# Transposing the first batch's deformable samples on TensorE through score banks

## The chip, the cores and the metric

The kernel runs on one core of one Trainium2 chip. The metric is device time in microseconds (us), lower is better, given as the median of several executions. Five engines work side by side, each with its own in-order queue of instructions: TensorE (PE; PEld is its weight load), VectorE (DVE), ScalarE (ACT), GpSimd (POOL) and SyncE (SP, which in this kernel issues nearly all DMAs). An instruction that waits holds up everything behind it on its engine.

## The reference

Four images of 128 channels and 64 x 64 positions go through two layers.

```python
x = x + deform(_gn(x), ...)                  # layer 0
t = _to_tokens(x)                            # [4, 4096, 128]
t = t + attn(_ln_t(t), ...)                  # layer 1
t = t + experts(_ln_t(t), ...)
...
# deform: offsets and a mask by two 3x3 convolutions, a bilinear sample of
# 128 channels at 9 shifted places per position, times the mask, then
out = jnp.einsum('bckhw,ock->bohw', samples, w_flat)
# attn: q = k = v = products of cosines of the 16 heads' 8 numbers
scores = jnp.einsum('bhsd,bhtd->bhst', q, q) / np.sqrt(D)
ctx = jnp.einsum('bhst,bhtd->bhsd', jax.nn.softmax(scores, axis=-1), q)
# then a projection, layer norms and a small feed-forward
# experts: softmax router over 8, the best two of them, weighted sum
```

All inputs and outputs are float32.

## The kernel before

**Tiling.** A batch is one image. Its 4096 positions are 8 *chunks* of 512 (`CH`), its 16 heads 4 groups of 4 (`NGRP`). A *run* is one (batch, group, query chunk) over a list of key blocks of 128; a *step* is one key block of a run. A step has four score matmuls (`scores`, L1261, into two tiles of the pool `ps_s`, each 2 x 512 columns wide; that pool has three such tiles, called score banks below), two exponentials on ScalarE (L1270) and four matmuls into the accumulator `acc` (`context`, L1281). Scores are issued two steps ahead of the sums (`LAG`). There are 3700 steps; some blocks of exponentials are not computed anew but turned by VectorE and handed to another chunk by way of DRAM (`turn` L1140, `etd`, L1214).

**Side work.** Around the steps two kinds of jobs run, as Python generators. `prepare(b)` makes keys and values of a batch: group norm, a table of image corners in DRAM, offsets (`offsets`), then `deform`. Its 96 *units*, 12 for each chunk (3 groups of taps x 4 blocks of 128 positions), each gather three taps by indirect DMA from POOL (L625), then multiply and add on VectorE (L645, L650, L651). `convolved` takes a chunk's 9 x 512 samples, channels on partitions (`sT`), and multiplies them with the weights (L754 to L757 by way of the helper line L281, 18 products of 256 columns), and `features` turns the result into queries, keys (`kTd`, `qTd`) and values (`fqd`) in DRAM, from where runs load them (L1239, L1241, L1249). `finish(b, ch)` is the rest of the network for a chunk whose sums are done: `attention_out`, `feed_forward`, `experts`. Two `finish` jobs may be open; they have rank 1 and 2.

**Samples.** Samples come with positions on partitions and have to be transposed. Batch 0's chunks 0 and 1 (`ch < 2`) take TensorE: three transposes into the one bank `misc`, held until VectorE copies it (L665) after the next unit's product. All others take a detour: VectorE transposes squares of 32 (L686) into `tr9`, SyncE stores that to `smd` in DRAM (L698, four stores for each group of taps) and loads it back in the other order (L731, `get`).

**The order of instructions** on PE, DVE, POOL and SP is written out by a planner in the kernel, the class `Beside`. It keeps its own clock (`now`, 1.82 us a step) and a time at which VectorE will be free (`dve`). A generator yields what it needs next (PE time, VectorE time, a delay); `step` emits it when it fits: VectorE's queue is no longer than `backlog`, a share `rate` of PE time has been saved up, at most `fills` jobs with PE work a step, and the bank `misc` is free, which `hold=True` reserves, and `hold=None` ignores. `later` emits a DMA at a due time. `force` runs a job when the next step's keys aren't there. After the last step `drain` emits what is left, one job to its end before the next.

**The opening.** In batch 0 the steps start before all chunks are prepared. The first 26 runs (`opening`, 160 steps; the flag `streaming`) work on the chunks 0 to 3 as they come: chunk 1 is wanted from step 16, chunk 2 from 64, chunk 3 from 104, chunks 4 to 7 from step 256. Partial sums are therefore parked in DRAM: at a run's end ScalarE copies `acc` to `cu` (L1491), SyncE stores it to `partd` 3 us later by the planner's clock (`park_sums`, L1126), and a later run of the same sums loads it at its first step (L1456) and adds it by four matmuls with the identity (L281, `acc<-cu`).

Of the kernel before, what the change touches and what calls it, by code (L numbers as in the profile page):

```python
# [22 lines left out]
P = 128  # L23
# [195 lines left out]
def tr(n):  # L219

    return 0.13 + 0.115 * n
# [3 lines left out]
def kernel(  # L225
# [373 lines left out]
    def deform(b, tab, idx, wt, rest):  # L599
# [7 lines left out]

        def early(n):

            return b == 0 and n < 3 * 12  # L610

        def gather(last):

# [20 lines left out]
        for n, (ch, kg, j) in enumerate(units):  # L634
            progress[b] = 0.1 + 0.9 * n / len(units)
            if b == 0 and n == 36:
                yield need(dve=5.0)
                settle()
            while not ahead:
                yield need(lat=0.5)  # L640
            v, landed = ahead.pop(0)
            v4 = v.rearrange("p k (q c) -> p (k q) c", c=C)
            w12 = wt[:, j, 3 * kg : 3 * kg + 3, :].rearrange("p k q -> p (k q)")
            yield need(dve=ve(1536), after=landed)
            nc.vector.tensor_tensor(v4, v4, w12[:, :, None].to_broadcast([P, 12, C]), ALU.mult)  # L645
            if moved:
                yield need(pe=0.01, dve=ve(384))
                moved.pop()()
            yield need(dve=ve(768) + ve(384))
            nc.vector.tensor_tensor(v[:, :, : 2 * C], v[:, :, : 2 * C], v[:, :, 2 * C :], ALU.add)  # L650
            nc.vector.tensor_tensor(v[:, :, :C], v[:, :, :C], v[:, :, C : 2 * C], ALU.add)  # L651
            if b == 0 and ch < 2:


                if n % 12 == 0:
                    while len(summed) < ch:
                        yield need(lat=0.5)
                    sT = big.tile([P, KK, CH], F32, tag="xs", name=f"sT_first{ch}")
                yield need(pe=tr(3), lat=FREE, hold=True)
                pt = misc(f"sT_ps{j}_{kg}")  # L660
                for k in range(3):
                    nc.tensor.transpose(pt[:, P * k : P * (k + 1)], v[:, k, :C], ident)

                def move(sT=sT, kg=kg, i=j % 4, pt=pt):
                    nc.vector.tensor_copy(  # L665
                        sT[:, 3 * kg : 3 * kg + 3, P * i : P * (i + 1)],
                        pt[:, : 3 * P].rearrange("p (k c) -> p k c", c=P),
                    )

                moved.append(move)  # L670
                beside.later(beside.now + 0.8, lambda n=n: gather(n))
                if n % 12 == 11:
                    yield need(pe=0.01, dve=ve(384))
                    moved.pop()()
                    featuring.append(True)
                    beside.add("prepare", convolved(b, ch, sT), 0.5, True)
                    if ch == 0:
                        yield from rest
                continue

            yield need(dve=ve(384))
            if j % 4 == 0:
                beside.flush(sent)
                tr9 = work.tile([P, 4, 4, 4, 32], F32, tag="st", name=f"tr{b}_{ch}_{kg}", bufs=NST)
            for k in range(3):
                nc.vector.transpose(  # L686
                    out=tr9[:, k, :, j % 4, :],
                    in_=v[:, k, :C].rearrange("p (c i) -> p c i", i=32),
                )
            beside.later(beside.dve, lambda n=n: gather(n))  # L690
            if j % 4 < 3:
                continue
            while kg == 0 and len(featuring) > 1:
                yield need(lat=1.0)

            def put(ch=ch, kg=kg, tr9=tr9):
                for o in range(4):
                    nc.sync.dma_start(  # L698
                        out=smd[ch % 2][:, 3 * kg : 3 * kg + 3, :, o].rearrange(
                            "i k c n -> i (k c) n"  # L700
                        ),
                        in_=tr9[32 * o : 32 * (o + 1), :3].rearrange("p k c j t -> p (k c) (j t)"),
                    )
# [15 lines left out]
    def convolved(b, ch, sT=None):  # L719
# [4 lines left out]
        if not in_order:  # L724
            yield need(lat=2.5)

            sT = big.tile([P, KK, CH], F32, tag="xs", name=f"sT{b}_{ch}")

        def get(kg):
            for c in range(4):  # L730
                nc.sync.dma_start(  # L731
                    out=sT[32 * c : 32 * (c + 1), 3 * kg : 3 * kg + 3],
                    in_=smd[ch % 2][:, 3 * kg : 3 * kg + 3, c].rearrange("i k o n -> i k (o n)"),
                )

# [5 lines left out]
        for k in range(KK):  # L741
            if k == 2 and not in_order:
                get(2)
            for hf in range(2):
                last = k == KK - 1 and hf == 1
                yield need(pe=MM256, dve=ve(128, 4) if last else 0.0, lat=0.2 if last else FREE, hold=not last)
                if k == 0 and hf == 0:
                    po = misc(f"conv_ps{b}_{ch}")
                by_columns(
                    po[:, 256 * hf : 256 * (hf + 1)], wconv_sb[:, k, :],  # L750
                    sT[:, k, 256 * hf : 256 * (hf + 1)], k == 0 and hf == 0, last,
                )
        summed.append(True)
        for o in range(4):  # L754
# [38 lines left out]
    def features(b, ch, x2, mean, rstd):  # L793
# [55 lines left out]
        beside.later(beside.dve - ve(512), lambda: put(0, hi))  # L849
        beside.later(beside.dve, lambda: put(1, lo))  # L850
        prepared[b, ch] = beside.dve + 9.0
        featuring.pop(0)

# [65 lines left out]

    def feed_forward(b, ch, x4, a4):  # L920

        z3 = [
            work.tile([P, 4, HD], F32, tag=f"zf{k}", name=f"zf{k}{b}_{ch}") for k in range(3)
        ]
# [29 lines left out]
        for i in range(4):  # L954
            for f in range(FFN // P):
# [164 lines left out]

        beside.later(beside.dve, put)

    def park_sums(g, sc, cu, when):

        def put():
            nc.sync.dma_start(out=partd[g][sc], in_=cu)  # L1126
            storing.discard((g, sc))

        storing.add((g, sc))
        beside.later(when, put)  # L1130

# [90 lines left out]

    landing = {}
    fetched = {}
    groups, done, active = {}, [], []

    def finishing():

# [179 lines left out]
    with tc.manual_schedule(engines={PE, DVE, SP, POOL}):  # L1410
# [6 lines left out]
        while n < len(steps):  # L1417
# [17 lines left out]
                    gives.remove(steps[m])  # L1435
                    turn(es[m - n], *steps[m])

            beside.fills = 3 if run < 12 else 1
            if streaming:
                backlog = 1.5  # L1440
            else:
                backlog = 0.4 if at >= len(ts) - 3 else 3.2
            if b + 1 < NB:
# [45 lines left out]
                cu = work.tile([P, 512], F32, tag="cu", name=f"cu{run}", bufs=NCU)  # L1489
            if by_act:  # L1490
                nc.scalar.copy(cu, acc)  # L1491
# [83 lines left out]
```

## Time and profile before

| | us |
|---|---|
| median of 3 executions | 7609.23 (7607.39 to 7621.65) |
| the profiled execution | 7579.71 |
| its span, first to last instruction | 7576.5 |
| ScalarE busy in it | 6863.5 |
| TensorE busy in it, as modelled | 7113.9 |
| first exponential starts at | 176.2 |
| steps 16, 20, 104, 160, 320 start at | 267.5, 287.6, 491.9, 637.0, 954.6 |
| last exponential starts at | 7490.8 |

A profile row has an engine, a line of the code, an operation, `out<-in` by the program's names, a count, and busy time. A row "A <- B: t, n, m" in the list of waits says that A waited for B t us in all, n times, at most m. A timeline row begins with its start and its length; in brackets stands the idle time before it and what ended that. Ends of matmuls are modelled, so TensorE's share looks fuller than it is. Matmuls in full float32 have two records each.

### The profile page before, as it was taken

The page shows a single profiled execution, that of the slowest core. Times are in us where ns is not written, and L with a number is a line of the kernel's source. Part 1 is how long each engine was busy: PE and PEld are TensorE (multiplying, and loading weights), DVE is VectorE, ACT ScalarE, POOL GpSimd, SP SyncE. Part 2 cuts the span into 40 slices and gives each one's busy share as a digit, 9 for nine tenths or more (in the row PEclk, how much of TensorE's full clock was granted, in tenths as well). Part 3 has the DMA queues.
Part 4 walks back from the last instruction along what each step waited for, and adds up shares of the span by engine and source line. Part 5 has one row for each costly group of instructions (what it writes and reads, how often), then busy time and mean ns, then how long its engine had stood idle before and what let it go on. Part 6 is the DMA issues. An engine that isn't in the chain of part 4 may idle for free.

```text
span 7576.5 us, 180754 instructions
## 1 busy us (share of the span) xinstructions
PE 7113.9 (94%) x73848; PEld 2375.9 (31%) x73848; DVE 4465.9 (59%) x8950; ACT 6863.5 (91%) x7467; POOL 1653.2 (22%) x1326
## 2 busy tenths in 40 slices
PE   3688999899999999999999999999999999999997
PEld 2122222223333333333333323333333333333333
DVE  7755356667444877776544677775444554455434
ACT  0578999889999999999999998989999999999995
POOL 5544034443000433422000334431000000000000
PEclk6889999999999999999999999999999999999998
DMA  6777567978446878887655789897454466666661
GB/s 181 223 204 219 141 223 241 300 234 291 149 168 200 292 244 280 268 277 244 203 179 190 228 279 298 289 324 237 174 190 152 148 236 230 232 222 239 226 202 63
DMA packets 909788, 1689.51 MB, mean 223 GB/s; under 512 B 150754, under 2 KB 384124, under 8 KB 858268
## 3 DMA queue, kind: packets, MB, share of 16 engines
q1 hardware_dynamic: 809102, 1371.37, 54.9%
q0 software_dynamic: 92160, 302.06, 12.4%
q8 instruction: 579, 9.49, 0.5%
q10 hardware_dynamic: 7694, 4.52, 0.2%
q14 instruction: 253, 2.07, 0.1%
HBM read 1027.51 MB, written 650.14 MB: 221 GB/s over the span
## 4 chain that ended last, share of the span: by engine, by line
PE 80%; DMA 8%; DVE 4%; issue 2%; ACT 2%; SPq 1%; another core or an unknown queue 0%; POOL 0%; POOLq 0%; DVEq 0%; ACTq 0%
PE acc L1281 39%; PE sc L1261 24%; PE acc L1214 5%; PE e_ps L281 4%; PE conv_ps L281 3%; DMA et<-etd 2%; PE f_ps L281 2%; ACT e L1270 2%; DMA etd<-st 1%; DMA sT<-smd 1%; PE om_ps L533 1%; DMA smd<-tr 1%; DVE st L1140 1%; DVE v L645 1%; DMA cu<-part 1%
## 5 line engine op out<-in xcount | busy, mean ns | idle before, releaser
L1270 ACT ACTIVATE e<-sc 128x1024 f32<-128x1024 f32 x7400 | 6849.4, 1081 | 527.0 <-PE sc L1261 368.1
L1281 PE MATMUL acc<-e,qf 128*9 128x512 f32 (+1 forms) x29600 | 3938.3, 601 | 18.6 <-ACT cu L1491 7.5
L1261 PE MATMUL sc<-qT,kT 32*128 32x512 f32 x14800 | 2368.7, 499 | 153.3 <-ACT e L1270 84.8
L1261 PEld LDWEIGHTS sc<-qT,kT 32*128 32x128 f32 x14800 | 942.8, 183 | 3612.6 <-ACT e L1270 3130.4
L625 POOL DMA_INDIRECT v<-tab,idx x1152 | 1451.8, 1260 | 1579.3 <-DVE tr L686 956.2
L1140 DVE STREAM_TRANSPOSE st<-e 128x1024 f32<-128x1024 f32 x792 | 937.3, 1222 | 752.4 <-ACT e L1270 620.1
L1281 PEld LDWEIGHTS acc<-e,qf 128*9 128x9 f32 (+1 forms) x29600 | 682.4, 91 | 610.3 <-issue 346.8
L396 POOL TENSOR_TENSOR r<-ln_t,expo 128x4 f32<-128x4 f32 x96 | 112.2, 1169 | 3105.4 <-DVE ln_t L394 3057.0
L645 DVE TENSOR_TENSOR v<-v,wt 128x1536 f32<-128x1536 f32 x384 | 667.0, 1737 | 119.5 <-DMA v<-tab,idx 96.8
L1214 PE MATMUL acc<-et,qv 128*9 128x128 f32 x12672 | 506.4, 276 | 52.2 <-DMA et<-etd 44.6
L1065 DVE TENSOR_TENSOR eo<-e_ps,gt 128x512 f32<-128x512 f32 x256 | 175.2, 686 | 552.5 <-PE e_ps L281 547.5
L650 DVE TENSOR_TENSOR v<-v 128x768 f32<-128x768 f32 x384 | 367.2, 956 | 10.1
L281 PE MATMUL conv_ps<-sT,wconv_sb 128*32 128x256 f32 x4320 | 351.0, 399 | 15.7 <-DMA sT<-smd 11.6
L1214 PEld LDWEIGHTS acc<-et,qv 128*9 128x9 f32 x12672 | 270.0, 90 | 254.4 <-issue 212.6
L686 DVE STREAM_TRANSPOSE tr<-v 128x128 f32<-128x128 f32 x1080 | 249.4, 282 | 37.5 <-DMA etd<-st 28.7
L1493 DVE COPY cu<-acc 128x512 f32<-128x512 f32 x116 | 80.2, 692 | 306.3 <-PE acc L1281 260.8
L651 DVE TENSOR_TENSOR v<-v 128x384 f32<-128x384 f32 x384 | 215.7, 562 | 13.3
L396 POOL TENSOR_TENSOR rstd<-lt_t,expo 128x4 f32<-128x4 f32 x32 | 57.9, 1811 | 575.9 <-DVE lt_t L394 550.7
L281 PE MATMUL f_ps<-w_sb,h 128*32 128x128 f32 x4096 | 166.1, 282 | 0.1
L950 DVE TENSOR_SCALAR h<-h_ps,b_sb 128x512 f32<-128x512 f32 x128 | 94.9, 744 | 100.3 <-PE h_ps L948 89.9
L823 POOL COPY fx<-rn 128x512 f32<-128x512 f32 x32 | 26.8, 838 | 526.3 <-DVE rn L822 321.4
L965 DVE TENSOR_TENSOR a<-a,f_ps 128x512 f32<-128x512 f32 x32 | 21.9, 685 | 198.8 <-PE f_ps L281 198.8
(227 smaller groups left out, 3166.9 us busy)
## 6 DMA issues: line engine op xcount, KB each, us to landing
etd<-st SPq DMA_DIRECT2D x396, 1024.0 KB
et<-etd SPq DMA_DIRECT2D x396, 1024.0 KB
kT<-kTd SPq DMA_DIRECT2D x372, 256.0 KB
smd<-tr SPq DMA_DIRECT2D x360, 192.0 KB
sT<-smd SPq DMA_DIRECT2D x360, 192.0 KB
qT<-qTd SPq DMA_DIRECT2D x166, 256.0 KB
atd<-cu SPq DMA_DIRECT2D x128, 256.0 KB
qf<-fqd SPq DMA_DIRECT2D x372, 72.0 KB
```

Source lines behind the costliest of these rows:

```text
L281: nc.tensor.matmul(dst[c : c + 32], lhsT=lhsT[:, c : c + 32], rhs=rhs, start=start, stop=stop)
L625: nc.gpsimd.indirect_dma_start(out=v[:, k, :], out_offset=None, in_=tab, in_offset=bass.IndirectOffsetOnAxis(ap=idx[:, j, kk : kk + 1], ax ...
L645: nc.vector.tensor_tensor(v4, v4, w12[:, :, None].to_broadcast([P, 12, C]), ALU.mult)
L650: nc.vector.tensor_tensor(v[:, :, : 2 * C], v[:, :, : 2 * C], v[:, :, 2 * C :], ALU.add)
L651: nc.vector.tensor_tensor(v[:, :, :C], v[:, :, :C], v[:, :, C : 2 * C], ALU.add)
L686: nc.vector.transpose(out=tr9[:, k, :, j % 4, :], in_=v[:, k, :C].rearrange("p (c i) -> p c i", i=32),)
L1065: nc.vector.tensor_tensor(ws[hf], pe.rearrange("p (e c) -> p e c", c=C), gt[:, i, 4 * hf : 4 * (hf + 1), None].to_broadcast([P, 4, C]), AL ...
L1140: nc.vector.transpose(out=st[:, :, 2 * pr : 2 * pr + 2, :].rearrange("p o h (q j) -> p o (h q) j", j=32), in_=es[pr].rearrange("p h (q o i ...
L1214: nc.tensor.matmul(acc[32 * h : 32 * h + QW, P * kt : P * (kt + 1)], lhsT=qv[:, at : at + QW], rhs=e[:, :, h, 32 * t : 32 * (t + 1)], star ...
L1261: nc.tensor.matmul(ps[i // 2][:, i % 2, :], lhsT=kT[h : h + 32, P * (t % 4) : P * (t % 4 + 1)], rhs=qT[h : h + 32, :], start=True, stop=True,)
L1270: nc.scalar.activation(e, ps[pr], AF.Exp, scale=1.0 / math.sqrt(HD))
L1281: nc.tensor.matmul(acc[32 * h : 32 * h + width, :], lhsT=flat[:, first : first + width], rhs=es[h // 2][:, h % 2, :], start=(t == ts[0]), ...
```

## The change

It has six parts.

1. All of batch 0's samples go through TensorE. The target of the transposes is a score bank of `ps_s` in place of `misc`, and VectorE copies it by three copies of 128 columns. Even chunks' samples lie in the one buffer `xs`, odd chunks' in nine of the eleven buffers `f2` that the finishing jobs use later; a chunk may start when the one two before it is summed.
2. In batch 0 the gathers run 4 units ahead throughout (before: in the first 36 units, 2 later), with the buffers `et` as additional space.
3. While streaming, `fills` is 3 (before: in the first 12 runs) and `backlog` 4.0 (before 1.5).
4. `features`: the values' copy moves from POOL to VectorE; its stores become one DMA for four, and those of keys and queries four for eight, with another order of the rows.
5. While streaming, the parked sums are stored by a DMA that ScalarE issues right after its copy.
6. Only one `feed_forward` at a time may be between its start and its second sum (`heavy`).

```diff
         def early(n):
-            return b == 0 and n < 3 * 12
+            return b == 0
...
             if moved:
-                yield need(pe=0.01, dve=ve(384))
+                yield need(dve=ve(128, 3))
                 moved.pop()()
...
-            if b == 0 and ch < 2:
+            if b == 0:
                 if n % 12 == 0:
-                    while len(summed) < ch:
+                    while len(summed) < ch - 1:
                         yield need(lat=0.5)
-                    sT = big.tile([P, KK, CH], F32, tag="xs", name=f"sT_first{ch}")
-                yield need(pe=tr(3), lat=FREE, hold=True)
-                pt = misc(f"sT_ps{j}_{kg}")
+                    if ch % 2:
+                        sT = [
+                            work.tile([P, CH], F32, tag="f2", name=f"sT{ch}_{k}", bufs=NF2)
+                            for k in range(KK)
+                        ]
+                    else:
+                        sT = big.tile([P, KK, CH], F32, tag="xs", name=f"sT_first{ch}")
+                        sT = [sT[:, k] for k in range(KK)]
+                yield need(pe=tr(3), lat=FREE, hold=None)
+                pt = ps_s.tile([P, 2, 512], F32, tag="sc", name=f"sT_ps{j}_{kg}")[:, 0, :]
                 for k in range(3):
                     nc.tensor.transpose(pt[:, P * k : P * (k + 1)], v[:, k, :C], ident)
                 def move(sT=sT, kg=kg, i=j % 4, pt=pt):
-                    nc.vector.tensor_copy(
-                        sT[:, 3 * kg : 3 * kg + 3, P * i : P * (i + 1)],
-                        pt[:, : 3 * P].rearrange("p (k c) -> p k c", c=P),
-                    )
+                    for k in range(3):
+                        nc.vector.tensor_copy(
+                            sT[3 * kg + k][:, P * i : P * (i + 1)], pt[:, P * k : P * (k + 1)]
+                        )
                 moved.append(move)
                 beside.later(beside.now + 0.8, lambda n=n: gather(n))
                 if n % 12 == 11:
-                    yield need(pe=0.01, dve=ve(384))
+                    yield need(lat=0.6)
+                    yield need(dve=ve(128, 3))
                     moved.pop()()
...
-        beside.later(beside.dve, lambda: nc.gpsimd.tensor_copy(f4[:, :, :, :HD], q8))
-        def put_values():
-            for g in range(NGRP):
-                nc.sync.dma_start(out=fqd[b % 2][ch][g], in_=fx[:, :, QG * g : QG * g + QL])
-        beside.later(beside.dve + 2.0, put_values)
-        yield need(pe=tr(4), dve=ve(512, 2))
+        yield need(pe=tr(4), dve=ve(512, 3))
...
         nc.vector.tensor_tensor(lo.bitcast(F32R), pt, hi, ALU.subtract)
+        nc.vector.tensor_copy(f4[:, :, :, :HD], q8)
         def put(part, fT):
-            kd = kTd[b % 2][ch].rearrange("(h l r d) n -> l r h d n", l=2, r=2, d=HD)
-            qd = qTd[b % 2][ch].rearrange("(h r l d) n -> l r h d n", l=2, r=2, d=HD)
-            for rep in range(2):
-                nc.sync.dma_start(out=kd[part, rep], in_=fT)
-                nc.sync.dma_start(out=qd[part, rep], in_=fT)
+            kd = kTd[b % 2][ch].rearrange("(p l r) n -> l p r n", l=2, r=2)
+            qd = qTd[b % 2][ch].rearrange("(p r l) n -> l p r n", l=2, r=2)
+            twice = fT[:, None, :].to_broadcast([P, 2, CH])
+            nc.sync.dma_start(out=kd[part], in_=twice)
+            nc.sync.dma_start(out=qd[part], in_=twice)
+        def put_values():
+            nc.sync.dma_start(
+                out=fqd[b % 2][ch].rearrange("g p t x -> p t g x"),
+                in_=fx.rearrange("p t (g x) -> p t g x", g=NGRP),
+            )
...
     def feed_forward(b, ch, x4, a4):
+        while heavy:
+            yield need(lat=1.0)
+        heavy.append(True)
...
         nc.vector.tensor_tensor(a4, a4, pf.rearrange("p (i c) -> p i c", c=C), ALU.add)
+        heavy.pop()
...
-            beside.fills = 3 if run < 12 else 1
+            beside.fills = 3 if streaming else 1
             if streaming:
-                backlog = 1.5
+                backlog = 4.0
...
             if by_act:
                 nc.scalar.copy(cu, acc)
+                nc.scalar.dma_start(out=partd[g][sc], in_=cu)
...
-            else:
-                park_sums(g, sc, cu, beside.now + 3.0 if by_act else beside.dve)
+            elif not by_act:
+                park_sums(g, sc, cu)
```

More of the change, by code (lines that the diff above doesn't have):

```diff
@@ L725, in convolved @@
             yield need(lat=2.5)
-            sT = big.tile([P, KK, CH], F32, tag="xs", name=f"sT{b}_{ch}")
+            sTs = big.tile([P, KK, CH], F32, tag="xs", name=f"sT{b}_{ch}")
+            sT = [sTs[:, k] for k in range(KK)]
         def get(kg):
@@ L731, in get @@
                 nc.sync.dma_start(
-                    out=sT[32 * c : 32 * (c + 1), 3 * kg : 3 * kg + 3],
+                    out=sTs[32 * c : 32 * (c + 1), 3 * kg : 3 * kg + 3],
                     in_=smd[ch % 2][:, 3 * kg : 3 * kg + 3, c].rearrange("i k o n -> i k (o n)"),
@@ L750, in convolved @@
                     po[:, 256 * hf : 256 * (hf + 1)], wconv_sb[:, k, :],
-                    sT[:, k, 256 * hf : 256 * (hf + 1)], k == 0 and hf == 0, last,
+                    sT[k][:, 256 * hf : 256 * (hf + 1)], k == 0 and hf == 0, last,
                 )
@@ L839, in features @@
         nc.vector.tensor_tensor(lo.bitcast(F32R), pt, hi, ALU.subtract)
+        nc.vector.tensor_copy(f4[:, :, :, :HD], q8)
         def put(part, fT):
-            kd = kTd[b % 2][ch].rearrange("(h l r d) n -> l r h d n", l=2, r=2, d=HD)
-            qd = qTd[b % 2][ch].rearrange("(h r l d) n -> l r h d n", l=2, r=2, d=HD)
-            for rep in range(2):
-                nc.sync.dma_start(out=kd[part, rep], in_=fT)
-                nc.sync.dma_start(out=qd[part, rep], in_=fT)
-        beside.later(beside.dve - ve(512), lambda: put(0, hi))
-        beside.later(beside.dve, lambda: put(1, lo))
+            kd = kTd[b % 2][ch].rearrange("(p l r) n -> l p r n", l=2, r=2)
[8 more added lines that the diff above has]
+            )
+        beside.later(beside.dve - 2.0 * ve(512), lambda: put(0, hi))
+        beside.later(beside.dve - ve(512), lambda: put(1, lo))
+        beside.later(beside.dve, put_values)
         prepared[b, ch] = beside.dve + 9.0
@@ L1121, in park_context, with park_sums @@
         beside.later(beside.dve, put)
-    def park_sums(g, sc, cu, when):
+    def park_sums(g, sc, cu):
         def put():
@@ L1129, in park_sums @@
         storing.add((g, sc))
-        beside.later(when, put)
+        beside.later(beside.dve, put)
     def turn(es, run, t):
@@ L1226 @@
     fetched = {}
-    groups, done, active = {}, [], []
+    groups, done, active, heavy = {}, [], [], []
     def finishing():
```

## The prediction

> **What bounds the kernel now.** I began with the page's totals and costliest groups.
>
> ```profile
> span 7576.5 us, 180754 instructions
> PE 7113.9 (94%) x73848; PEld 2375.9 (31%) x73848; DVE 4465.9 (59%) x8950; ACT 6863.5 (91%) x7467; POOL 1653.2 (22%) x1326
> L1270 ACT ACTIVATE e<-sc 128x1024 f32<-128x1024 f32 x7400 | 6849.4, 1081 | 527.0 <-PE sc L1261 368.1
> ```
>
> One step of attention is two exponentials (ACT) fed by four score matmuls (PE). There are 3700 steps, 6849.4 / 3700 = 1.85 us of ACT each, and this set of steps is not touched. So the span is 1.85 us per step, plus whatever time ACT stands idle: 7576.5 - 6863.5 = 713 us. The change can win only there. Where does it lie in the part the change rewrites, batch 0's preparation? Busy time by window (after the times: PE, PEld, DVE, ACT, POOL, clock, DMA share, GB/s):
>
> ```profile
> 267.00:288.00 21.00, 12.46 (x62) 2.86 (x58) 16.06 (x35) 8.56 (x10) 12.73 (x11) 0.66 1.06 322
> 288.00:640.00 352.00, 297.18 (x2338) 84.24 (x2338) 213.82 (x387) 274.14 (x304) 169.99 (x131) 0.88 0.73 219
> 640.00:880.00 240.00, 233.93 (x1868) 66.23 (x1864) 121.43 (x248) 231.25 (x252) 60.40 (x46) 0.98 0.55 158
> ```
>
> ACT is idle 12 + 78 = 90 us between 267 and 640, but only 9 us from 640 to 880, though preparation still runs there. The list of waits for 288 to 640 (total, times, longest), and SyncE's queue for 160 to 640, say why:
>
> ```profile
> PE acc L281 <- DMA cu<-part: 16.4, 4, 6.6
> PE sc L1261 <- DMA kT<-kTd: 13.8, 1, 13.8
> PEld acc L281 <- DMA cu<-part: 20.3, 4, 7.5
> SPq L1126 <- ACT cu L1491: 105.1, 14, 19.9
> ```
>
> TensorE waits 36.7 us for parked sums to come back (cu; another 7.2 us at 284) and 13.8 us for chunk 3's keys. SyncE itself stood 105 us in front of the stores of such sums. Its timeline around step 104, and ACT's row after it:
>
> ```profile
> 478.00 2.96 SPq L698 DMA_DIRECT2D smd<-tr  x4
> ...
> 486.60 9.39 SPq L731 DMA_DIRECT2D sT<-smd  x8
> 496.30 0.34 SPq L1456 DMA_DIRECT2D cu<-part  x1
> ...
> 509.71 0.58 ACT L1491 COPY cu<-acc 128x512 f32<-128x512 f32 x1 [9.43 <-PE acc L281]
> ```
>
> The load of the sums (496.3) is issued behind eight loads of samples that took SyncE 9.4 us, and ACT then idles 9.4 us. All this is the traffic of the DRAM detour.
>
> **What the change removes.** The detour of batch 0: for chunks 2 to 7, 12 stores (L698) and 12 loads (L731) of 192 KB each, and with the stores to ACT's queue the 105 us of SyncE's waiting. Of the 43.9 us of cu waits I leave 10, since the loads themselves still share the DMA engines: -34 (bounds -44 and -10). Chunk 3's 13.8 us: its keys were issued only after the smd stores at 478 to 481; -12 (0 to -14).
>
> Chunk 1, for which TensorE waits 22.0 us until 266.6: eight stores of its features take SyncE from 248.2 to 254.7, now four, about -3. A POOL copy that stood 9.8 us in front of the gathers goes. Against it, VectorE's copy out of PSUM was one of 384 columns (L665, 0.55 us) and becomes three of 128; the row like that is L1007 (128x128 from PSUM, 0.29), so 0.87 - 0.55 = 0.32 x 24 units = +7.7 us where VectorE is 83% busy (166.49 of 200 us from 100 to 300). The longer VectorE queue can fill some of the other 33 us. Taken -3, from -10 to +8. For chunks 2 to 7 three copies replace three stream transposes (L686, 0.28): nothing. The features' copy moves from POOL to VectorE at 0.69 us a chunk, beside VectorE's slack (59% busy): nothing; with the slack gone it would be 32 x 0.69 = 22.
>
> A rule speaks against the split: the Trainium skill (Perfetto Trace Analysis, Optimizing Scalar/DVE Operations) puts about 125 ns of access overhead on each VectorE instruction on PSUM and advises fewer, larger ones. By it two more cost 0.25 a unit, 6.0 us in place of 7.7, and the sum would be 2 lower.
>
> **What it adds to TensorE and ACT.** (a) Three convolution products in a step instead of one. Timeline of TensorE, with three, and then two score rows of steps with one:
>
> ```profile
> 302.77 0.51 PE L1261 MATMUL sc<-qT,kT 32*128 32x512 f32 x4
> 303.21 1.50 PE L281 MATMUL conv_ps<-sT,wconv_sb 128*32 128x256 f32 x24
> 304.53 1.04 PE L1281 MATMUL acc<-e,qf 128*9 128x512 f32 x8
> 305.50 0.51 PE L1261 MATMUL sc<-qT,kT 32*128 32x512 f32 x4
> ...
> 425.24 0.51 PE L1261 MATMUL sc<-qT,kT 32*128 32x512 f32 x4
> 427.11 0.51 PE L1261 MATMUL sc<-qT,kT 32*128 32x512 f32 x4
> ```
>
> A step lasts 2.73 us with three products and 1.87 with one; one without any is bound by ACT, at 1.85. In the built order of instructions chunks 2 to 5 now have six steps of three each; before, chunk 2 alone had five of three and one of two (2.29 us, 308.23 to 310.52), the others one each: 24 x 0.86 - (5 x 0.86 + 0.42) = +15.9. (b) 26 stores issued by ACT; SyncE's row for them (L1126) is 0.34 each: +8.8. In steps of (a) ACT waits anyway, which hides some of (b): together +20 (8 to 25).
>
> (c) 72 more units are transposed by TensorE. Four transposes took 0.60 us (rows of L765), so three 0.45. Taking the eight records of a product (0.57 us, from the chain of waits) out of 1.87 leaves 1.30 us of PE for a bare step against 1.85 of ACT, so 0.45 hides; and in the built order none of the 63 units transposed after step 16 stands in a step with a convolution product. Nothing; where the cover is gone, 72 x 0.45 = 32. (d) The target is now one of the three score banks, kept until the three copies, which stand behind the next unit's product (1.75 us) in VectorE's queue: 1.75 + 0.87 = 2.6 us, or about 4.5 where features' instructions come between. Meanwhile scores alternate on two banks, and TensorE, whose queue is in order, stops at the transposes, and every score and sum behind them, when VectorE is late (gathers held VectorE 26 times, 50.3 us, from 176 to 860; four ahead instead of two should lessen that). No row shows a borrowed bank. Below: 0, as TensorE can fill one bank while ACT empties the other. Above: the bare step's spare 0.55 us lost for each of the 72, 40, and 5 for late gathers: 45. Taken +10, nearer the lower end because the transposes stand in bare steps.
>
> **The tail.** Only one chunk may now be in the feed-forward at a time. In the built order this leaves the experts of batch 3's chunk 5 undone when the scores end; the second of two finishing jobs is starved and comes after chunk 7's last copy, on every engine. Rows of the last chunk's own experts, on VectorE:
>
> ```profile
> 7503.93 0.69 DVE L892 COPY y_6T<-y_ps 128x512 f32<-128x512 f32 x1 [0.57 <-PE y_ps L890]
> 7504.54 0.54 DVE L1097 RECIPROCAL rd<-rd 128x64 f32<-128x64 f32 x1
> ...
> 7547.02 0.29 DVE L1007 COPY lT<-l_ps 128x128 f32<-128x128 f32 x1 [0.78 <-PE l_ps L1002]
> ...
> 7572.14 0.69 DVE L892 COPY y_7T<-y_ps 128x512 f32<-128x512 f32 x1 [0.57 <-PE y_ps L890]
> ```
>
> Such a set takes 7572.83 - 7547.02 = 25.8 us, and nothing else runs then. Chunk 6 has some 1.5 blocks of experts fewer left, so the reciprocal need not wait for 7504.5 but for its load, issued at 7496.9: about -4.5. Together +21 (15 to 26).
>
> **The other batches.** 24 more chunks lose seven SyncE issues each and the POOL copy; ACT's idle time there (42 us from 2000 to 3000, 40, then 84) is mostly TensorE's side work, which stays. Taken -5 (-20 to +15).
>
> **Sum.** -34 - 12 - 3 + 20 + 10 + 21 - 5 = -3 us. The profiled execution took 7579.71 (span 7576.5 and 3.2 around it), 29.5 below the median of the three runs, 7609.23; the difference is added to that median: 7606.
>
> **Rivals.** *SyncE's queue was the whole trouble and the banks cost nothing* (faster): -44 - 14 - 3 + 20 + 0 + 21 - 15 = -35, 7574. For it: ACT is 96% busy from 640 to 880 beside one convolution product a step. Against it: 72 new places where TensorE waits for VectorE. *Borrowed banks hold up the scores* (slower): 45 in place of 10, +32, 7641. It decides once most banks are held for more than the 2.6 us of one product and three copies. For it: the 4.5 us case, and VectorE, whose chunk (12 x 4.1 us of units and about 19 of features, 69 us) must now fit in some 40 steps or 75 us. *The cu waits stay* (slower), because the load is slow in the DMA engines (73% busy) and not in SyncE's queue: -10 in place of -34 and 0 in place of -12, +33, 7642. For it: on the chain of waits single loads of cu take 12.5 and 13.0 us. Against it: the 105 us in SyncE's row, and that the sample traffic leaves the DMA engines too.
>
> The Trainium skill (DMA: Bandwidth & Descriptors, Issuing engines are not separate DMA queues) speaks for the last: issuing from another engine saves only the issuer's time. By it the moved stores give SyncE 26 x 0.34 us and no more, and the sum would be that rival's.
>
> **Chances.** No change as summed (own range 7590 to 7622): 0.40; SyncE the whole trouble 0.28; banks held 0.18; cu waits stay 0.14. A measurement of this kernel can tell about 0.2%, 15 us, from no change. Faster, below 7594: 0.27 of the second case and 0.09 of the first, 0.36. Slower, above 7624: 0.16, 0.12 and 0.05, 0.33. Between: 0.31. The range of 8 in 10 goes from 7568, a little under the fast rival, to 7648, a little over the two slow ones.
>
> **What would show it.** In the new profile: TensorE's waits for cu<-part before 640 near 10 us; step 160 (637.0 us before) some 15 to 25 us earlier; steps of 2.73 us in chunks 2 to 5; score matmuls waiting for the copies of sT seldom and shortly (right), or tens of times for half a microsecond and more (banks held); about 26 us of VectorE's work after chunk 7's last copy. The prediction is wrong if that tail is missing, or if ACT idles between steps 20 and 160 as much as now.

## The result and the profile after

| us | before | after |
|---|---|---|
| median | 7608.31 (7599.73 to 7621.65, 4 runs) | 7685.17 (7678.06 to 7700.96, 4 runs) |
| ratio, 95% interval | | 1.0102 (1.0079 to 1.0126) |
| span of the profiled execution | 7576.5 | 7676.2 |

The change costs 77 us where -3 was forecast. First the page's totals and costliest groups of the kernel after.

```profile
span 7676.2 us, 180662 instructions
PE 7177.9 (94%) x74064; PEld 2410.6 (31%) x74064; DVE 4464.0 (58%) x9030; ACT 6874.6 (90%) x7467; POOL 1589.3 (21%) x1294
L1284 ACT ACTIVATE e<-sc 128x1024 f32<-128x1024 f32 x7400 | 6859.2, 1072 | 602.1 <-PE sc L1275 419.5
```

VectorE and ScalarE do as much as before. What grew is ScalarE's idle time. To see where, I took the start of each step from the exponentials' rows, in this profile, the first one of before and a second one of before (one of the runs below, 7620.42 us, since the first lay at the fast end of all its runs):

| us | step 160 at | step 320 at | 320-760 | 760-1750 | 1750-2500 | 2500-2640 | 2640-3699 | last exponential to end |
|---|---|---|---|---|---|---|---|---|
| before, first profile | 637.0 | 954.6 | 911.6 | 1914.4 | 1496.1 | 259.2 | 1954.0 | 84.6 |
| before, second | 652.5 | 971.4 | 913.8 | 1927.4 | 1506.4 | 259.2 | 1954.2 | 84.2 |
| after | 634.5 | 955.5 | 924.1 | 1954.9 | 1494.6 | 284.9 | 1954.5 | 105.8 |

Two executions of the kernel before differ by 17 us up to step 320 and by 26 from there to 2640; the last three columns repeat within half a microsecond. Against the second profile the rewritten opening gains 16 us (against the first it gains nothing). Against the second profile all is lost later, in stages whose code hardly changed: 10 + 28 us from 320 to 1750, 26 from 2500 to 2640, 22 in the tail, against 12 won back from 1750 to 2500.

In the opening, the windows that were shown of before, now of the kernel after (columns as there):

```profile
288.00:640.00 352.00, 306.99 (x2485) 96.74 (x2484) 224.65 (x438) 278.23 (x305) 158.68 (x128) 0.95 0.56 173
640.00:880.00 240.00, 223.80 (x1795) 65.17 (x1791) 112.01 (x221) 222.31 (x240) 54.12 (x46) 0.97 0.42 128
```

The DMA share fell from 0.73 to 0.56, so the detour's traffic is gone, but ScalarE still idles 74 us of the 352, and now 18 of the next 240, where it was 9. The waits of that stretch (288 to 640) in the kernel after, and SyncE's queue in 160 to 640:

```profile
PEld acc L281 <- DMA cu<-part: 11.3, 1, 11.3
PE acc L281 <- DMA cu<-part: 10.4, 1, 10.4
PEld sT_ps L669 <- ACT e L1284: 14.2, 20, 1.2
PEld sc L1275 <- DVE sT_first L673: 2.0, 3, 0.9
SPq L777 <- DVE x L776: 97.9, 5, 31.9
SPq L1263 <- PE sc L1275: 72.8, 11, 17.3
SPq L849 <- DVE hiT L840: 49.7, 4, 21.5
SPq L1470 <- DMA part<-cu: 43.6, 5, 16.3
```

No wait for keys is left, and one wait for parked sums, which is listed twice (below). Scores hardly wait for the copies of borrowed banks: 2.0 us in the row shown. And SyncE, freed of the 105 us in front of ScalarE's copies, now stands 98 us in front of the residual's store (L777; 11 before) and 50 in front of the keys' (L849), both for VectorE, 73 in front of loads of queries (L1263; no such row before) until scores have freed a buffer, and 44 in front of loads of sums (L1470; 17 before) until the sums' stores have landed. The timeline up to the one long wait for sums, SyncE's rows and then TensorE's:

```profile
437.09 0.37 SPq L849 DMA_DIRECT2D kTd<-hiT  x1
...
441.50 5.87 SPq L1470 DMA_DIRECT2D cu<-part  x1
...
454.75 1.93 PE L281 MATMUL acc<-cu,ident 128*32 128x512 f32 x8 [10.39 <-DMA cu<-part]
```

The keys' store could go only at 437.09, 21.5 us after SyncE came to it; the load of the sums stands behind it, and TensorE waited 10.4 us, until 454.75, for that load. The head of the queue changed, not the queue.

The tail of the kernel after, VectorE's rows of the last experts:

```profile
7620.88 0.29 DVE L1021 COPY lT<-l_ps 128x128 f32<-128x128 f32 x1 [0.78 <-PE l_ps L1016]
...
7646.29 0.69 DVE L902 COPY y_7T<-y_ps 128x512 f32<-128x512 f32 x1 [0.57 <-PE y_ps L900]
7646.91 0.29 DVE L1021 COPY lT<-l_ps 128x128 f32<-128x128 f32 x1
...
7672.30 0.69 DVE L902 COPY y_5T<-y_ps 128x512 f32<-128x512 f32 x1 [0.57 <-PE y_ps L900]
```

Chunk 5's experts come after chunk 7's, as the built order said: 26 us. Its cause turned out to be another one than forecast.

### The profile page after: what moved, and what is told of

Its sections match the earlier page's. It is cut to its first block, busy times and chain, and to the rows that moved or that the text cites. A ratio compares the mean times of both kernels' runs of the same rounds, so it can differ in the third digit from the quotient of the medians.

```text
span 7676.2 us, 180662 instructions
## 1 busy us (share of the span) xinstructions
PE 7177.9 (94%) x74064; PEld 2410.6 (31%) x74064; DVE 4464.0 (58%) x9030; ACT 6874.6 (90%) x7467; POOL 1589.3 (21%) x1294
## 4 chain that ended last, share of the span: by engine, by line
PE 84%; DMA 6%; DVE 3%; ACT 3%; issue 2%; SPq 1%; another core or an unknown queue 1%; POOL 0%; ACTq 0%; POOLq 0%; DVEq 0%
PE acc L1295 40%; PE sc L1275 25%; PE acc L1228 6%; PE conv_ps L281 4%; PE e_ps L281 3%; ACT e L1284 3%; PE f_ps L281 2%; DMA et<-etd 2%; DMA sT<-smd 1%; PE om_ps L533 1%; DVE v L645 1%; PE ao_ps L281 0%; POOL v L625 0%; PE sT_ps L669 0%
## 5 line engine op out<-in xcount | busy, mean ns | idle before, releaser
L625 POOL DMA_INDIRECT v<-tab,idx x1152 | 1423.4, 1236 | 2143.1 <-DVE tr L694 1202.3
L281 PE MATMUL conv_ps<-sT,wconv_sb 128*32 128x256 f32 x4032 | 324.3, 398 | 27.3 <-DMA sT<-smd 22.7
L694 DVE STREAM_TRANSPOSE tr<-v 128x128 f32<-128x128 f32 x864 | 199.3, 281 | 21.6 <-DMA etd<-st 14.9
L669 PE MATMUL sT_ps<-ident,v 128*128 128x128 f32 x288 | 63.8, 341 | 117.8 <-DVE v L651 76.1
```

What stands on the lines that cost most here:

```text
L281: nc.tensor.matmul(dst[c : c + 32], lhsT=lhsT[:, c : c + 32], rhs=rhs, start=start, stop=stop)
L625: nc.gpsimd.indirect_dma_start(out=v[:, k, :], out_offset=None, in_=tab, in_offset=bass.IndirectOffsetOnAxis(ap=idx[:, j, kk : kk + 1], ax ...
L694: nc.vector.transpose(out=tr9[:, k, :, j % 4, :], in_=v[:, k, :C].rearrange("p (c i) -> p c i", i=32),)
```

## The experiments

The runs stand on five chips (7, 13, 5, 8 and 10 on record), each with the kernel before beside them. On the first three, for the first twelve runs, it took 7605.13, 7607.41 and 7609.43 us, as in the result, and medians are compared as they are. On chip 8 it took 7459.42 us and on chip 10 7581.88, so times there are compared by their ratio to before. Profiles of one kernel differ too, as the two of before show, so a stretch that is some 15 us longer in one profile proves little by itself.

### Part 4 and the lock, undone and alone

On chip 7. `a_nofeat`: the changed kernel with `features` of before. `b_heavy`: the kernel before with the lock alone. `b_dma`: the kernel before with the merged DMAs alone:

```diff
-            for rep in range(2):
-                nc.sync.dma_start(out=kd[part, rep], in_=fT)
-                nc.sync.dma_start(out=qd[part, rep], in_=fT)
+            twice = fT[:, None, :].to_broadcast([P, 2, CH])
+            nc.sync.dma_start(out=kd[part], in_=twice)
+            nc.sync.dma_start(out=qd[part], in_=twice)
```

`a_heavy02`: the changed kernel with `while heavy and b < NB - 1:`.

> The changed kernel with the features as before (part 4 undone: POOL makes the values' copy again, twelve DMAs instead of five). Theory F, the merged DMAs and the copy on VectorE cost the later batches their +55 us between steps 320 and 2640: about 7635 us, step 2640 some 50 us earlier than in the changed kernel. Theory L, the lock of the feed-forward costs it: 7685 within 10, step 2640 unchanged. Theory R, the planner's order after step 320 is merely another one and its cost a matter of chance: a shift of either sign, up to 30 us. The tail after the last exponential stays near 106 us in all three.

> The kernel before with part 6 alone (the lock of the feed-forward). Theory L: steps 320 to 2640 take some 50 us longer and the tail grows from 86 to about 107 us, 7670 to 7685 us. Theory F: only the tail grows, 7630 us. Theory R: the tail grows, and the steps shift by up to 30 us either way, 7600 to 7660.

> The kernel before with the merged DMAs of part 4 alone (POOL keeps the values' copy). Theory F: steps 320 to 2640 take 30 to 50 us longer, 7640 to 7660 us. Theory L: 7608 within 8. Theory R: 7608 within 30 either way, with no wait for kT, qf or qT that is new.

> The changed kernel with the lock lifted for the last batch. If the starved job of batch 3's chunk 5 makes the longer tail: last exponential to end falls from 106 to about 86 us, and 22 us go, 7663 us. Theory L: in addition steps up to 2640 stay as slow as in the changed kernel, since the lock still holds in batches 0 to 2. If the tail has another cause: 7685 within 8.

| | median | ratio (interval) | tail |
|---|---|---|---|
| a_nofeat | 7622.19 | 1.0020 (1.0009 to 1.0031) | 84.3 |
| b_heavy | 7639.00 | 1.0049 (1.0032 to 1.0065) | 89.8 |
| b_dma | 7631.48 | 1.0033 (1.0020 to 1.0045) | 85.0 |
| a_heavy02 | 7673.54 | 1.0090 (1.0074 to 1.0107) | 107.0 |

Undoing part 4 takes 63 us away, near theory F's 50, but not where theory F put them: between the two profiles step 320 comes 21 us sooner, steps 320 to 2640 are only 11 us shorter, and, against all three theories, the long tail goes with it. The merged DMAs alone cost 26 us in the kernel before. The lock costs 34 us alone, but hardly in the tail (+5); its clearest loss is in steps 760 to 1750 (1942.4, in the two profiles of before 1914.4 and 1927.4), where the finishing of batch 0 now drags on (its last experts at step 1750 in place of 1737). Lifting the lock in the last batch leaves the tail at 107.0 with the experts of every chunk at the same step, chunk 5's still last: the starved job has nothing to do with the lock. That falsifies the prediction's cause of the tail, with its size right.

### Which piece of part 4: DMAs or the copy

On chip 13. `a_olddma` has the twelve small DMAs in the changed kernel, VectorE keeping the copy; `a_poolcopy` the reverse, the diff of it:

```diff
-        yield need(pe=tr(4), dve=ve(512, 3))
+        beside.later(beside.dve, lambda: nc.gpsimd.tensor_copy(f4[:, :, :, :HD], q8))
+        yield need(pe=tr(4), dve=ve(512, 2))
...
-        nc.vector.tensor_copy(f4[:, :, :, :HD], q8)
```

`a_nofeat_h0` is `a_nofeat` with `while heavy and b == 0:`, and `before_again` the kernel before.

> The kernel before once more, unchanged, for a second profile. Its first profile lay 29.5 us below the median of its runs. If executions differ by chance all along: a span near 7602 us, with the difference spread over steps 0 to 1750 and an unchanged tail of 85 us. If the first one was fast in one place, that place shows.

> The changed kernel with the twelve small DMAs of the features in place of the five merged ones; VectorE keeps the values' copy, and the order of everything else is the changed kernel's. Theory D, the merged DMAs cost by themselves (26 us in the kernel before): 7685 - 26 = 7659 us, the delay gone before step 320, the tail still 106 us and the last features still at step 2640. Theory V, the copy's place on VectorE and the order that follows from it cost all of the 63 us: 7685 within 8.

> The changed kernel with the values' copy on POOL again and the merged DMAs kept; the order of the side work is then that of the run without part 4. Theory D: 7622 + 26 = 7648 us, tail 85 us, no loss at steps 2500 to 2640. Theory V: 7622 us within 8.

> The changed kernel without part 4 and with the lock of the feed-forward held in batch 0 alone. If the lock costs by itself in batches 1 to 3 (34 us in the kernel before): 7590 to 7600 us, and with that faster than before. If its cost was the order of that kernel alone: 7622 within 10.

`a_olddma`: 7705.12, 1.0123 (1.0106 to 1.0140), tail 106.8. `a_poolcopy`: 7634.43, 1.0035 (1.0023 to 1.0047), tail 84.6. The merged DMAs are not the loss: putting the small ones back in the same order takes nothing away (20 more by the medians, with intervals that overlap), though in the kernel before merging them cost 26. What goes with the copy is: `a_poolcopy` is 51 us quicker than the changed kernel and has the short tail. `a_nofeat_h0`: 7627.79, 1.0024 (1.0015 to 1.0034), no gain; the traces show why: its order on TensorE is that of `a_nofeat` up to step 1851, after batch 0's last experts, and the lock's loss lies before that.

### The copy, or what the planner is told of it

The copy changed two things: an instruction moved to VectorE's queue, and the planner was told of three VectorE operations (2.11 us by its `ve`) in place of two (1.41), after which it chooses another order. These can be separated, on chip 5. `a_quiet` keeps the copy on VectorE and tells two; `a_ghost` has it on POOL and tells three. TensorE's order in `a_quiet` is that of `a_poolcopy` instruction for instruction, in `a_ghost` that of the changed kernel.

```diff
-        yield need(pe=tr(4), dve=ve(512, 3))
+        yield need(pe=tr(4), dve=ve(512, 2))
...
-        beside.later(beside.dve - 2.0 * ve(512), lambda: put(0, hi))
-        beside.later(beside.dve - ve(512), lambda: put(1, lo))
-        beside.later(beside.dve, put_values)
+        beside.later(beside.dve - ve(512), lambda: put(0, hi))
+        beside.later(beside.dve, lambda: put(1, lo))
+        beside.later(beside.dve + 0.7, put_values)
```

> The changed kernel, VectorE making the values' copy, but with the planner told of two VectorE operations in place of three at that point: TensorE's and ScalarE's order are those of the run with the POOL copy (7634 us), VectorE's too but for the copy itself. Theory O, the copy's cost lies in the order that the planner makes when it is told of it: 7634 within 8, tail 85 us, no loss at steps 2500 to 2640. Theory X, the copy in VectorE's queue itself delays what is behind it: 7685. A mixture: step 320 as late as in the changed kernel (some 20 us after the POOL run), tail 85 us, 7655 us.

> The counterpart: POOL makes the values' copy, but the planner is told of three VectorE operations, so the order on TensorE and ScalarE is the changed kernel's. Theory O: 7685 within 8, tail 106 us and the loss at steps 2500 to 2640 as in the changed kernel. Theory X: 7634. Mixture: tail 106 us, step 320 some 20 us earlier than in the changed kernel, 7665 us.

| median us, ratio (interval) | copy on POOL | copy on VectorE |
|---|---|---|
| told two | 7634.43, 1.0035 (1.0023 to 1.0047) | 7604.63, 0.9999 (0.9988 to 1.0011) |
| told three | 7671.42, 1.0077 (1.0060 to 1.0095) | 7685.17, 1.0102 (1.0079 to 1.0126) |

The instruction itself on VectorE (with the values' store due a little sooner) costs nothing that can be shown: it is 30 us *cheaper* with two told, on two chips, and 14 dearer with three, where the intervals overlap. By the medians the order costs 37 us with the copy on POOL and 81 with it on VectorE, as much as all of the change's loss: told of two, the changed kernel is even with the kernel before. Two parts of this cost, 43 us in all, repeat at fixed places: in all five profiles with that order (the changed kernel's two, `a_ghost`, `a_olddma`, and `a_heavy02`, which has it up to step 3658) steps 2500 to 2640 take 282 to 285 us (263.5 in `a_quiet`) and the tail 105.6 to 107.0 (83.9). In that order the last batch's finishing trails: chunk 4's experts end at step 3614, in `a_quiet` at 3559, and chunk 5's, at step 3669 there, no longer fit in before the last step. Windows of that stretch, first the kernel after, then `a_quiet`:

```profile
5329.00:5614.00 285.00, 269.46 (x2900) 90.68 (x2901) 160.46 (x324) 260.09 (x284) 40.25 (x34) 0.98 0.72 233
```

```profile
5293.00:5556.00 263.00, 259.71 (x3004) 88.93 (x2996) 145.33 (x290) 258.46 (x281) 24.85 (x20) 1.00 0.70 231
```

In these 140 steps the new order has more of batch 3's preparation to do (POOL 34 instructions against 20, VectorE 15 us more), and ScalarE idles 25 us in place of 5. One of its waits, in the timeline of the kernel after:

```profile
5504.09 1.04 PE L1228 MATMUL acc<-et,qv 128*9 128x128 f32 x16 [6.48 <-DMA et<-etd]
...
5507.60 1.94 ACT L1284 ACTIVATE e<-sc 128x1024 f32<-128x1024 f32 x2 [7.97 <-PE sc L1275]
```

A load of handed-over exponentials is late, TensorE stops for 6.5 us, and ScalarE for 8.0. This is step 2582, which takes 6.4 to 8.7 us more than 1.85 in all five profiles and nothing more in `a_quiet`.

### Without the lock

Two unlocked finishing jobs share the buffers `f2`; here there are twelve (the twelfth was not tried alone). On chip 5 too, `a_nofh12` is `a_nofeat` without the lock, `a_pool12` is `a_poolcopy` without it.

```diff
-NF2 = 11
+NF2 = 12
...
-        while heavy:
-            yield need(lat=1.0)
-        heavy.append(True)
...
-        heavy.pop()
```

> The changed kernel without part 4 and without the lock of part 6, with twelve f2 buffers in place of eleven so that two finishing jobs can go side by side. If the lock is what slows steps 760 to 1750 (27 us more there than the kernel before's second profile has, 34 us for the lock alone in the kernel before): 7590 to 7600 us, steps 760 to 1750 at some 1930 us as in the kernel before. If it is not: 7622 within 8 and steps 760 to 1750 at 1955 to 1962.

> The same with the merged DMAs kept (POOL copy, no lock, twelve f2 buffers). If the lock costs: 7634 less 20 to 34, 7600 to 7614 us. If not: 7634 within 8. The merged DMAs by themselves, read against the run without part 4 and lock: +12 as with the lock, or +26 as in the kernel before.

`a_nofh12`: 7601.41, 0.9995 (0.9985 to 1.0005). `a_pool12`: 7609.99, 0.9998 (0.9983 to 1.0013). So the lock costs 21 and 24 us, in the place that was named: steps 760 to 1750 take 1921.2 and 1935.6 in place of 1962.1 and 1959.0 (those on other chips, but `a_quiet`, locked and on this one, takes 1953.6). The merged DMAs, with the same order on TensorE, cost 9 us here and 12 with the lock, neither clear of noise. Without the lock, part of the gain goes elsewhere (2500 to 2640 take 279.6 and 284.2 in place of 260.9 and 264.7). Parts 1, 2, 3 and 5 together, which `a_nofh12` holds, thus bring nothing that can be measured (-8 us), though step 320 is 20 to 37 us earlier than in the two profiles of before.

### Does the order always cost; do the gains add; the clusters

On chip 8. `q_free`: `a_quiet` without the lock, twelve buffers. `b_ghost12`: the kernel before, only told three in place of two, twelve buffers. `q_told25`: `a_quiet` told `ve(512, 2.5)`. `q_fills`: `a_quiet` with `beside.fills = 3 if run < 12 else 1`, as before the change.

> All parts of the change but the lock, with twelve f2 buffers, VectorE making the values' copy and the planner told of two operations there. If the lock's 21 to 24 us (7622 to 7601, 7634 to 7610) and the copy's 30 us (7634 to 7605) add: 7583 us, 0.3% faster than before. Its preparation of batch 3 ends at step 2652, so 20 us should be lost at steps 2500 to 2640, as in the two other runs without the lock. If the gains don't add: 7600 to 7605.

> The kernel before with one number changed: the planner is told of three VectorE operations in place of two at the features (POOL still makes the copy), and twelve f2 buffers so that the order can run. No instruction is added or taken away. Theory O, the order alone costs: preparation of batch 3 ends at step 2661, some 20 us lost at steps 2500 to 2640, 7630 to 7650 us. If the order mattered only together with the rest of the change: 7608 within 8.

> The run with two operations told, now with two and a half told (1.75 in place of 1.40 us). By the built order the preparation of batch 3 ends at step 2490 in place of 2621. If being told more is what costs, by later and longer gaps: between 7605 and 7685, some 7640. If what costs is where the order happens to put the preparation of batch 3 and the last chunks: no loss at steps 2500 to 2640, tail 85 us, 7600 within 10.

> The run with two operations told, and the side products again at most one in a step after run 12 (part 3 partly undone; the backlog stays at 4.0). If the clusters of three products cost the 16 to 20 us that the prediction summed: step 320 that much earlier, about 928, and 7587 us. If they cost nothing on balance, since chunks come sooner by them: step 320 at 946 or later, 7605 or more.

| | median | ratio (interval) | step 160 at | step 320 at | 2500-2640 | tail |
|---|---|---|---|---|---|---|
| before | 7459.42 | | | | | |
| q_free | 7424.80 | 0.9951 (0.9934 to 0.9967) | 602.5 | 917.4 | 270.1 | 80.8 |
| b_ghost12 | 7463.05 | 1.0004 (0.9995 to 1.0014) | 634.5 | 944.8 | 278.9 | 78.1 |
| q_told25 | 7477.68 | 1.0027 (1.0015 to 1.0038) | 603.0 | 915.3 | 258.1 | 86.9 |
| q_fills | 7440.35 | 0.9971 (0.9960 to 0.9981) | 581.5 | 912.5 | 258.1 | 92.4 |

`b_ghost12` contradicts a general reading of theory O: its preparation of batch 3 ends late too and it loses some 20 us at 2500 to 2640, but it ends even, so they are made good elsewhere. And `q_told25`, whose order has neither the late preparation nor the long tail, does not come out ahead. So being told more is not costly as such; each order meets its own collisions. `q_fills` against `q_free` (the lock first alters the order at step 1132, so up to step 320 only the clusters differ) shows what three products in a step cost: 21.0 us by step 160, of which 4.9 are left at step 320, since the products that were put off still have to be done.

On chip 10 the changed kernel was run again, with a last combination, `q_free` with `q_fills`' edit:

> The changed kernel once more, unchanged, since the runs of the last call had another chip, on which the kernel before takes 7459 us. If the order's cost of the first chip (1.0102 against 0.9999 with two operations told) holds there too: a ratio near 1.010. If the order costs less where transfers are quicker, as b_ghost12 (1.0004) suggests: 1.000 to 1.006. The tail of 106 us and the loss at steps 2500 to 2640 come from the order of instructions and should be there either way.

> The version without the lock and with two operations told (0.9951), and one side product in a step after run 12 (0.9971 against 1.0027 or 0.9999 with three). If the two gains add: 0.990 to 0.993. If the products only come later, as their steps 160 to 320 showed: 0.995 within 0.003.

`after_again`: 7645.79 against 7581.88, 1.0086 (1.0071 to 1.0102), with 282.6 us at steps 2500 to 2640 and a tail of 105.6: the loss goes with the order, not with the first chip. `q_free_fills`: 7580.36, 0.9994 (0.9984 to 1.0004): no gain over the kernel before is left. Since neither `q_free` nor `q_fills` ran on that chip, it stays open whether the combination or the chip takes the gains away. These two are the versions that beat the kernel before, by 0.5 and 0.3%, on the one chip where they ran.

## Why the prediction was wrong

**The failed step: "The features' copy moves from POOL to VectorE at 0.69 us a chunk, beside VectorE's slack (59% busy): nothing".** The instruction was priced, and too high (it took 0.42 us). What it does to the planner was left out of the sum: told of 0.70 us more, 32 times, it lays out every step after 48 anew. Two pairs of runs that differ in what is told put that at 37 and 81 us, and 43 us stand at the same places in every profile with that order. With it fell **"The other batches ... Taken -5 (-20 to +15)"**: steps 320 to 3699 take 52 us longer than in the second profile of before (6613.0 against 6561.0), 78 longer than in the first. The built order was at hand, and I used it for the tail alone.

**The tail, +21: size right (21.6), cause wrong.** It was read off the built order correctly, but laid to part 6; lifting the lock changed nothing, telling two took it away.

**The lock** was priced through the tail alone. It costs 21 to 34 us in three pairs of runs, while batch 0 is finished.

**"The cu waits: -34", mis-sized: -13.** The sum 16.4 + 20.3 counted each wait twice, once for the matmul and once for its weight load. TensorE's timeline of the kernel before:

```profile
284.54 1.93 PE L281 MATMUL acc<-cu,ident 128*32 128x512 f32 x8 [7.24 <-DMA cu<-part]
401.33 1.64 PE L281 MATMUL acc<-cu,ident 128*32 128x512 f32 x8 [3.27 <-DMA cu<-part]
523.92 1.06 PE L281 MATMUL acc<-cu,ident 128*32 128x512 f32 x8 [1.32 <-DMA cu<-part]
588.54 1.94 PE L281 MATMUL acc<-cu,ident 128*32 128x512 f32 x8 [5.20 <-DMA cu<-part]
604.53 1.93 PE L281 MATMUL acc<-cu,ident 128*32 128x512 f32 x8 [6.57 <-DMA cu<-part]
```

That is five waits, 23.6 us (six of 24.7 in the second profile), of which one of 10.4 is left. That 10 were left, as forecast, is luck: the reason given was the load's share of the DMA engines, and what shows is a load behind a store in SyncE's queue. None of the five stands near 509.71, where I laid ScalarE's 9.4 us to such a load: there TensorE had waited 3.8 us for samples and then done convolution products. "With the stores to ACT's queue the 105 us of SyncE's waiting" go was right to the letter and worth little, since 98 and 50 us of waiting for VectorE, 73 for a free buffer and 44 for stores to land took their place. That also settles the rivals: "SyncE's queue the whole trouble" fell, and "the cu waits stay" was half right.

**Chunk 3's keys, -12: right in kind.** The wait is gone; it was 13.8 us in one profile of before and 6.1 in the other.

**Borrowed banks, +10: no such cost shows.** In 288 to 640 scores waited 2.0 us for the copies. Instead the transposes wait for ScalarE to free a bank, 14.2 us in 20 waits, none over 1.2; while ScalarE is the one waited for, this need not cost it anything. The banks were not tried alone.

**Clusters, with the stores +20: right by step 160 (21.0 for the clusters), wrong at the end (4.9 by step 320).** Work that was moved forward was counted as work added. ScalarE's stores were not tried alone.

**The opening in sum** was -19 (-34 - 12 - 3 + 20 + 10) and came to -16 against the second profile of before (+1 against the first), by terms that were wrong both ways, so the agreement is luck. Chunk 1's -3 cannot be told from noise: step 16 starts at 264.6, in the two profiles of before at 267.5 and 279.0.

**The split copy out of PSUM, +7.7 with VectorE short of time: size right.** Three copies of 128 columns take 0.282 us each and one of 384 took 0.551, so 0.30 more a unit. The Trainium skill (Perfetto Trace Analysis, Optimizing Scalar/DVE Operations) puts the access overhead of one VectorE instruction on PSUM at about 125 ns; two more of them would be 0.25, an estimate that is close. What the split cost on the path was not tried alone.

**The signs.** The tail came, of another cause; steps of 2.73 us came (products start at 381.90, 384.63 and so on to 395.53). Step 160 comes 18 us sooner than in the second profile of before, as forecast, but only 2.5 sooner than in the first. One of the two signs of being wrong came as well: between steps 20 and 160 ScalarE idles 77.2 us, as much as before (77.9 and 82.1).

What stays open is how the new order loses more than the tail (22) and the stretch at 2500 to 2640 (21). Of the 80 us between its profile and that of `a_quiet` the other 36 are 10 by step 320, 13 in 320 to 760 and 12 in 1750 to 2500, with next to nothing in the rest. The last two cannot be laid to the order: `a_poolcopy`, with the order of `a_quiet`, takes 924.6 and 1493.8 us there, as long as the changed kernel (924.1 and 1494.6), and the changed kernel's second profile, on chip 10, takes 911.1 and 1482.9, as short as `a_quiet` (911.0 and 1482.6). `b_ghost12` and `q_told25` show that no rule of "late preparation" foretells the total.

## What to carry to other kernels

Where a planner decides the order, a changed cost estimate is an edit of the whole program: compare the built orders to the end, and separate the instruction from what the planner is told of it by two runs. A wait shown for a matmul and for its weight load is one wait. Freeing a queue of one blocker gains only what the next one leaves, and work moved forward is not work added.

## Not expected of the hardware

The same kernel before took 7605 to 7609, 7459 and 7582 us on different chips, while steps 2640 to 3699, where ScalarE hardly idles, took 1952 to 1962 us in every profile. Where the quickest chip differs is in small stalls. Between 1310 and 7000 us the score weight loads waited with no releaser shown, in the second profile of before and then in `b_ghost12` (same instructions in another order, chip 8):

```profile
PEld sc L1261 <- issue: 296.5, 352, 2.5
```

```profile
PEld sc L1261 <- issue: 69.7, 68, 1.7
```

It is the chip and not the order: all four profiles of chip 8 have 64 to 71 us of this, the sixteen of the other chips 274 to 312, at granted clocks that hardly differ (0.99 in both of these, 1310 to 7000). What causes the 280 more of them was not tried. The copy of 512 columns into a strided view took VectorE 0.42 us, and POOL 0.84 on average (median 0.61).
